# Attention's probabilities in units of 512 columns, and scores written further ahead of the values

## The chip, the cores and the metric

The kernel runs on one core of one Trainium2 chip. A core has a matrix engine (TensorE, shown as PE, and as PEld for its weight loads), a vector engine (DVE), a scalar engine (ACT), GpSimd (POOL) and SyncE (SP), which here issues most DMAs. The metric is the device time of one launch in microseconds; the time of a kernel is the median of its runs.

## The reference, cut to what matters

All arrays are float32; `x` is 2 sequences of 2048 tokens with 256 features. A feed-forward layer with three experts stands before and after a causal attention with one head of 128 features:

```python
x = x + 0.5 * _L0_ffn_ref(_layernorm(x), ...)      # three experts, one wins each token
x = x + _L0_attn_ref(_layernorm(x), Wq, Wk, Wv, Wo)
x = x + 0.5 * _L0_ffn_ref(_layernorm(x), ...)      # the same weights again

def _L0_attn_ref(x, Wq, Wk, Wv, Wo):
    Q = x @ Wq
    K = x @ Wk
    V = x @ Wv
    logits = jnp.einsum('bqd,bkd->bqk', Q, K) * d_k ** (-0.5)
    logits = jnp.where(causal, -jnp.inf, logits)
    attn = jax.nn.softmax(logits, axis=-1)
    out = jnp.einsum('bqk,bkd->bqd', attn, V)
    return out @ Wo
```

In the feed-forward layer each token's three bids are computed from a gated mix of its normalized row; the expert with the highest bid is applied to it. Experts 0 and 1 are squared-ReLU networks with 1024 hidden features, expert 2 is a gated product with 256.

## The kernel before, in words

A tile has 128 tokens, a group has 4 tiles (512 tokens), a sequence has 4 groups. The program is one long list that Python generators write out. Each generator yields between its steps, and a driver decides in which order steps of several generators are written. Tile, the layer that builds the program, then gives each engine its own order: it goes through the list with a model of the durations, the written order is the priority, and an instruction may be put on its engine ahead of others that were written earlier. On the chip each engine takes its instructions in the order that was fixed there. Two calls hold instructions in place: `tc.keep_in_program_order(ins)` keeps one in its written place, and `tc.issue_after(ins)` (in the helper `behind`) puts those of a block behind `ins` on that engine.

**The feed-forward layer.** `front` works through the 8 groups of the two sequences. For each it normalizes the rows (`start`, `norm1`, which writes the columns `YN` of the group's `rows` tile), transposes them (`columns`), multiplies (`r`, `v`, `mix`), computes the bids (`route`, `logits`), chooses the winner (`choose`, whose last decision is the `wins` at L525), ranks the tokens per expert and scatters the rows by indirect DMA to `by_slot` in DRAM (`move`). `experts` works on blocks of up to 256 gathered rows: SyncE loads the rows, `ready` updates them (on VectorE L975, on ScalarE L976), `columns` transposes them, `first` makes the hidden features, `second` multiplies back and scatters the result to DRAM. Blocks of expert 2 are of the kind `gt`; there `first` ends with the product `gated` (L994), which `back_to_rows` (L877) multiplies next. The experts of the first sequence are written between the steps of the second sequence's front. Toward the end of the first layer, `ahead` fetches the first sequence's rows back from `x_mid`, one of its steps to three of the experts', and `normed` normalizes them for attention; `moments` computes each group's statistics with four `bn_stats` (L281). With `landing`, the first of these four is kept in its written place.

**Attention.** It runs for one sequence at a time. For the first it is written alone; for the second its steps are written between those of the next layer's front, nine of the front for eight of attention's.

- `qkv` makes the projections, two steps for each of the 4 groups. The first sequence uses the `YN` columns of the four `rows` tiles as its normalized input (`normed`); the second normalizes into `xn`, with two buffers.
- `scores` makes the probabilities of one query tile a step. Tile i of group n has n + 1 key chunks of up to 512 columns. Each chunk is a matmul into a bank `ps_s` (L1125) of the pool `p_mm`, which has 6 banks, also used by projections and sums. The last chunk is masked (L1133). VectorE takes each chunk's maximum (L1134), then that of the row (L1137) and its shift (L1138); ScalarE writes the exponentials to `prob` (L1141) and their sums; VectorE adds these up (L1150) and inverts them (L1152). `prob` is a tile of 128 x 2048, with 5 buffers, whatever the group.
- `values` goes through the key blocks of 128, of which group n has 4(n + 1). For a block it transposes the four query tiles' probabilities (L1165) into a bank of `p_tp`, copies this to `p_tr` (on VectorE for even blocks, L1172, on ScalarE for odd ones, L1170) and multiplies by the block's values (L1178). The transposes and the copy of a block are written one block ahead of its multiplication. After the second block the group before is finished (`sums`: L1194, L1200, L1205), in two steps.

The end of `attention` sets the written order. The first group's four score tiles stand in the last four steps of `qkv`. Those of group n + 1 stand among the steps of the values of group n, one after every n + 1 steps:

```python
side = scores(n + 1, seq, following) if n + 1 < GB else iter(())
for i, _ in enumerate(values(n, seq, probs)):
    if i % (n + 1) == n:
        next(side, None)
    yield
```

Of the kernel before, what the change touches and what calls it, by code (L numbers as in the profile page):

```python
# [8 lines left out]
F32 = mybir.dt.float32  # L9
# [7 lines left out]
P = 128  # L17
# [61 lines left out]
def kernel(ctx: ExitStack, tc: tile.TileContext, a: dict, out: bass.AP):  # L79
# [196 lines left out]
    def moments(src, landing=False):  # L276

        stats = small.tile([P, TB, 6], F32, name="stats")
        mv = small.tile([P, TB, 2], F32, name="mv")
        for t in range(TB):  # L280
            ins = nc.vector.bn_stats(stats[:, t, :], src[:, t, :])  # L281
            if landing and t == 0:
                tc.keep_in_program_order(ins)
        for t in range(TB):
            nc.vector.bn_aggr(mv[:, t, :], stats[:, t, :])
        return mv
# [80 lines left out]

    groups = []


    RW_AT, GT_AT, HALF_AT, MORE_AT, STEER = accumulate(POS, POS, POS, SQ, 1)

    class Group:
# [136 lines left out]
        def choose(self):  # L510
            upto = self.seg["upto"]
            if self.n == 0 and self.seg["prior"] is not None:
# [11 lines left out]
            nc.vector.tensor_tensor(wins[:, 2, :], bids[:, 2, :], most[:, 0, :], ALU.is_gt)  # L524
            nc.vector.scalar_tensor_tensor(  # L525
                wins[:, 1, :], wins[:, 0, :], 1.0, wins[:, 2, :], ALU.is_lt, ALU.subtract
            )
            for t in range(TB):
# [300 lines left out]
    def experts(work, segs, dest, redo=None):  # L829
# [118 lines left out]
        class Block:  # L948
# [35 lines left out]

            def first(self, following=None):

                if self.kind == "gt":
# [3 lines left out]
                    if following:  # L991
                        following.ready()
                    self.mid = work.tile([P, KC, BLK], F32, name="gated", bufs=2)
# [21 lines left out]
        def pipelined(todo):  # L1015
# [7 lines left out]
            yield  # L1023
            todo[0].ready()
            todo[0].columns()
            yield
            for i, block in enumerate(todo):
                if i + 1 < len(todo):
                    todo[i + 1].load_weights()
                if i + 2 < len(todo):  # L1030
                    todo[i + 2].load_rows()
                yield from block.first(todo[i + 1] if i + 1 < len(todo) else None)
                if i + 1 < len(todo):
                    todo[i + 1].columns()
                    yield
                yield from block.second()
# [29 lines left out]

    def attention(work, x, normed=()):

        stat = work

        def qkv(made):
# [6 lines left out]
            def begin(n):  # L1078
                if len(norms) <= n < GB:
                    xn = work.tile([P, TB, C], F32, name="xn", bufs=2)  # L1080
                    norms.append((xn, normalize(xn, x[n])))
                    next(norms[n][1])
# [31 lines left out]

        def scores(n, seq, probs):

            for i in range(TB):
                qi = n * TB + i
                prob = work.tile([P, T], F32, name="prob", bufs=5)
                top = stat.tile([P, GB], F32, name="top", bufs=6)  # L1120
# [18 lines left out]
                sums = stat.tile([P, GB], F32, name="sums", bufs=6)  # L1139
                for c, (ps, w) in enumerate(parts):  # L1140
                    nc.scalar.activation(  # L1141
                        prob[:, c * TG : c * TG + w],
                        ps[:, :w],
                        AF.Exp,
# [5 lines left out]
                nc.vector.reduce_sum(total, sums[:, : n + 1], axis=AX.X)  # L1150
                inv = stat.tile([P, 1], F32, name="inv", bufs=10)
                nc.vector.reciprocal(inv, total)  # L1152
                probs.append((prob, inv))
                yield

        def values(n, seq, probs):
            ps_o = p_mm.tile([P, TG], F32, name="ps_o", tag="mm")
            blocks = (n + 1) * TB

            def keys_first(j):  # L1160
# [3 lines left out]
                for i in range(i0, TB):  # L1164
                    nc.tensor.transpose(  # L1165
                        ps[:, i * P : (i + 1) * P], probs[i][0][:, j * P : (j + 1) * P], ident
                    )
# [8 lines left out]
            for j in range(blocks):  # L1176
# [11 lines left out]
                yield  # L1188
            left.append(sums(n, ps_o, probs))

        def sums(n, ps_o, probs):

# [3 lines left out]
            for t0 in range(0, TB, 2):  # L1196
# [6 lines left out]
                for i in range(2):  # L1203
                    t = t0 + i
                    nc.vector.scalar_tensor_tensor(  # L1205
                        x[n][:, t, :], ps[:, i, :], probs[t][1], x[n][:, t, :], ALU.mult, ALU.add
                    )
            yield

        seq, probs, left = {}, [], []  # L1210

        first_scores = scores(0, seq, probs)
        for i, _ in enumerate(qkv(seq)):
            if i >= GB:
                next(first_scores)
            yield
        yield from first_scores
        for n in range(GB):
            following = []
            side = scores(n + 1, seq, following) if n + 1 < GB else iter(())  # L1220
            for i, _ in enumerate(values(n, seq, probs)):
                if i % (n + 1) == n:
                    next(side, None)
                yield
            yield from side
            probs = following
        yield from left.pop()
# [87 lines left out]
    with pool("attention", "right") as work:  # L1315
        for n in range(GB):
            x = front_pool.tile([P, TB, C], F32, name=f"x{n}")
            wait_for(nc.sync.dma_start(x, token_tiles(x_mid, GB + n)).ins, s0["results"] + s1["results"])
            t1["x"].append(x)
        run(attention(work, t0["x"], [r[:, :, YN : YN + C] for r in t0["rows"]]))  # L1320
        following = front(front_pool, [t0, t1], by_exp=GB)
        interleave(attention(work, t1["x"]), until_placed(following, t0), 9, 8)
        advance(following, AHEAD)
# [49 lines left out]
```

## Time and profile before

| what | value |
|---|---|
| time before, median of 3 runs | 892.63 us (891.55 to 897.54) |
| the profiled execution, its own time | 900.5 us |
| its span, first to last instruction | 898.5 us |
| mean granted TensorE clock | 0.988 |
| first sequence's attention on TensorE, first transpose to last product | about 342 to 467 us |
| second sequence's attention, with the next front | about 467 to 642 us |

The profile is one execution; busy times are per engine, and idle time is told for the instruction that ended it, with what released it. Start times are in us from the start of the span. A float32 matmul stands as two instructions in the records, a transpose as one; ends of matmuls are modelled, so the records of neighbouring matmuls overlap.

### The profile page before, as it was taken

The numbers are of one execution on the slowest core, as the hardware profiler recorded it, in microseconds if no ns is written. First come the engines' busy times: TensorE is split into PE (matmuls) and PEld (weight loads), VectorE is DVE, ScalarE is ACT, GpSimd is POOL, SyncE is SP. The second block draws the span as 40 slices with busy tenths as digits, with TensorE's granted clock in tenths as the row PEclk, the third lists the DMA queues.
The fourth block names the chain that finished last, engine by engine and source line by source line (L and its number), as shares of the span: only waits on it lengthen the run. The fifth ranks groups of instructions, "written<-read, shape, count | busy, mean of one in ns | idle before, by whom it ended". The sixth has DMA issues, their size and how long they took to land. (4 is left out here: it accounts for less than half of the span.)

```text
span 898.5 us, 12471 instructions
## 1 busy us (share of the span) xinstructions
PE 846.5 (94%) x4136; PEld 616.5 (69%) x4136; DVE 467.4 (52%) x1857; ACT 320.1 (36%) x694; POOL 184.8 (21%) x232
## 2 busy tenths in 40 slices
PE   6999899999999998899899999999899899999996
PEld 4556467788878895545456556556566688888885
DVE  3688757333345445478532687675776532333322
ACT  3332541324344332344533344442352223243221
POOL 3145245111032211000000102022323410122101
PEclk9999999999999999999999999999999999999998
DMA  9425637647188543000000001021375654539642
GB/s 308 150 102 194 224 142 264 216 136 264 49 293 296 171 142 100 0 1 1 0 1 1 1 0 71 24 95 42 127 279 182 242 191 161 177 95 333 199 164 70
DMA packets 66370, 123.71 MB, mean 138 GB/s; under 512 B 4718, under 2 KB 44526, under 8 KB 66288
## 3 DMA queue, kind: packets, MB, share of 16 engines
q1 hardware_dynamic: 55856, 87.46, 29.0%
q0 software_dynamic: 8384, 33.70, 9.5%
q10 hardware_dynamic: 2048, 1.58, 0.6%
q8 instruction: 37, 0.61, 0.3%
q14 instruction: 45, 0.37, 0.1%
HBM read 82.47 MB, written 38.68 MB: 135 GB/s over the span
## 5 line engine op out<-in xcount | busy, mean ns | idle before, releaser
L877 PE MATMUL acc<-w_e,hid 128*128 128x256 f32 x704 | 158.2, 382 | 0.0
L862 PE MATMUL ps_b<-cols,w_k 128*128 128x256 f32 (+1 forms) x768 | 157.3, 363 | 0.0
L862 PEld LDWEIGHTS ps_b<-cols,w_k 128*128 128x128 f32 x768 | 137.4, 191 | 17.1
L877 PEld LDWEIGHTS acc<-w_e,hid 128*128 128x128 f32 x704 | 132.7, 192 | 17.9 <-DVE hid L1004 0.6
L291 POOL TENSOR_TENSOR r<-ve,mhalf 128x4 f32<-128x4 f32 (+1 forms) x40 | 50.9, 1272 | 383.0 <-DVE ve L332 264.4
L1003 ACT ACTIVATE relu<-ps_b 128x512 f32<-128x512 f32 x88 | 52.0, 591 | 179.5 <-PE ps_b L862 155.9
L1004 DVE TENSOR_TENSOR hid<-ps_b,relu 128x512 f32<-128x512 f32 x88 | 60.8, 691 | 84.8 <-ACT relu L1003 79.3
L902 DVE SCALAR_TENSOR_TENSOR res<-acc,rows_in 128x256 f32<-128x256 f32 x68 | 30.0, 478 | 123.9 <-PE acc L877 123.9
L1178 PE MATMUL ps_o<-p_tr,v 128*128 128x512 f32 (+3 forms) x160 | 75.2, 554 | 4.7 <-DVE p_tr L1172 1.9
L567 POOL DMA_INDIRECT by_slot<-rows,slots x64 | 62.5, 977 | 32.0 <-issue 27.0
L1141 ACT ACTIVATE prob<-ps_s,shift 128x512 f32<-128x512 f32 (+2 forms) x80 | 49.0, 621 | 53.8 <-DVE shift L1138 44.5
L1125 PE MATMUL ps_s<-k_t,q_t 128*128 128x512 f32 (+3 forms) x160 | 64.8, 533 | 0.9 <-ACT prob L1141 0.9
L910 POOL DMA_INDIRECT out_dram<-res,where x34 | 33.6, 987 | 155.4 <-DVE res L902 142.3
L362 PE MATMUL ps_p<-y_t,w_r 128*128 128x512 f32 x128 | 63.5, 615 | 0.8 <-ACT y_t L416 0.7
L362 PE MATMUL ps_p<-y_t,w_v 128*128 128x512 f32 x128 | 62.2, 605 | 0.0
L910 POOL DMA_INDIRECT x_mid<-res,where x34 | 33.7, 992 | 133.2 <-DVE res L902 128.0
L442 PE MATMUL acc<-w_o,gate_t 128*128 128x256 f32 x256 | 60.1, 385 | 0.6 <-DVE gate_t L432 0.6
L1165 PEld LDWEIGHTS ps_pt<-ident,prob 128*128 128x128 f32 x272 | 34.1, 143 | 36.9 <-issue 18.8
L1134 DVE TENSOR_REDUCE top<-ps_s 128x1 f32<-128x512 f32 (+2 forms) x80 | 48.4, 607 | 17.2 <-PE ps_s L1125 15.8
L442 PEld LDWEIGHTS acc<-w_o,gate_t 128*128 128x128 f32 x256 | 47.1, 190 | 8.6 <-DVE gate_t L432 1.4
L1125 PEld LDWEIGHTS ps_s<-k_t,q_t 128*128 128x128 f32 x160 | 29.9, 193 | 32.8 <-issue 24.7
L354 ACT ACTIVATE cols<-ps_bt,lnp 128x256 f32<-128x256 f32 (+1 forms) x96 | 47.2, 554 | 13.2 <-PE ps_bt L846 12.9
(219 smaller groups left out, 1128.1 us busy)
## 6 DMA issues: line engine op xcount, KB each, us to landing
w_k<-in_K_rwkv_dram SPq DMA_DIRECT2D x24, 1024.0 KB, 5.3
w_e<-in_V_rwkv_dram SPq DMA_DIRECT2D x24, 1024.0 KB, 5.8
rows_in<-by_slot SPq DMA_DIRECT2D x20, 516.0 KB, 6.6
rows_in<-by_slot SPq DMA_DIRECT2D x12, 772.0 KB, 6.6
rows<-in_x_dram SPq DMA_DIRECT2D x8, 512.0 KB, 5.9
by_slot<-rows_in SPq DMA_DIRECT2D x3, 772.0 KB, 10.5
x_mid<-rows_in SPq DMA_DIRECT2D x1, 2048.0 KB, 15.8
rows<-x_mid SPq DMA_DIRECT2D x4, 512.0 KB, 5.1
```

The lines of the kernel that those rows point to most:

```text
L291: guess = nc.gpsimd.tensor_tensor(r0[:, 0:n, :], ve[:, 0:n, :], mhalf[:, 0:n, :], ALU.pow)
L362: nc.tensor.matmul(ps, lhsT=w[:, k, m * P : (m + 1) * P], rhs=src_t[:, k, :], start=k == 0, stop=k == KC - 1)
L442: nc.tensor.matmul(acc[:, i, :], lhsT=self.gate_t[:, k, t * P : (t + 1) * P], rhs=w_o[:, k, :], start=k == 0, stop=k == KC - 1,)
L567: nc.gpsimd.indirect_dma_start(out=by_slot, out_offset=bass.IndirectOffsetOnAxis(ap=self.slots[:, t : t + 1], axis=0), in_=self.rows[:, t, :],
L862: nc.tensor.matmul(ps[:, j, :], lhsT=w[:, k, (m0 + j) * P : (m0 + j + 1) * P], rhs=cols[:, k, :], start=k == 0, stop=k == KC - 1,)
L877: nc.tensor.matmul(acc[:, i, :], lhsT=src[:, j, i * P : (i + 1) * P], rhs=w[:, j, :], start=j == 0, stop=j == n - 1,)
L910: ins = nc.gpsimd.indirect_dma_start(out=dest, out_offset=bass.IndirectOffsetOnAxis(ap=where[:, i : i + 1], axis=0), in_=res[:, i, :], in_ ...
L1003: nc.scalar.activation(relu, ps, AF.Relu)
L1004: self.made = nc.vector.tensor_mul(self.mid[:, j : j + step, :], ps, relu).ins
L1125: nc.tensor.matmul(ps[:, :w], lhsT=seq["q_t"][:, qi * P : (qi + 1) * P], rhs=seq["k_t"][:, c * TG : c * TG + w], start=True, stop=True,)
L1141: nc.scalar.activation(prob[:, c * TG : c * TG + w], ps[:, :w], AF.Exp, bias=shift, scale=ATTN_SCALE, accum_out=sums[:, c : c + 1],)
L1178: nc.tensor.matmul(ps_o[:, i0 * P :], lhsT=seq["v"][:, j, :], rhs=p_tr[:, i0 * P :], start=j == 0, stop=j == blocks - 1,)
```

## The change

- The five whole rows `prob` become 20 tiles `prob0` to `prob19` of 128 x 512 (`units`), of the same size in all, shared by both sequences. `homes` gives each query tile of group n exactly n + 1 of them, or halves of other tiles: in the fourth group two query tiles use four pieces of `spare`. In the first sequence these are halves of the normalized rows of groups 0 and 1, in the second the two `xn` tiles.
- `scores` is one generator over all 16 query tiles. Six are written in `qkv`, from its third step on. The other ten are written at steps given as a list for the values of each group: three, four, three and none.
- `inv` has 12 buffers for 10.
- With `landing`, all four `bn_stats` are kept in their written place.
- `ready` for the first two blocks of `experts` is put behind the most recent `wins` of L525.

```diff
@@ moments
-            if landing and t == 0:
+            if landing:
                 tc.keep_in_program_order(ins)
@@ Group.choose
-            nc.vector.scalar_tensor_tensor(
+            lately["chosen"] = nc.vector.scalar_tensor_tensor(
                 wins[:, 1, :], wins[:, 0, :], 1.0, wins[:, 2, :], ALU.is_lt, ALU.subtract
-            )
+            ).ins
@@ Block.first, and pipelined
-            def first(self, following=None):
+            def first(self, following=None, early=False):
...
                     if following:
-                        following.ready()
+                        following.ready(lately["chosen"] if early else None)
...
-            todo[0].ready()
+            todo[0].ready(lately["chosen"])
...
-                yield from block.first(todo[i + 1] if i + 1 < len(todo) else None)
+                yield from block.first(todo[i + 1] if i + 1 < len(todo) else None, i == 0)
@@ attention
-    def attention(work, x, normed=()):
+    def attention(work, x, units, spare, normed=()):
+        homes = [[units[i : i + 1] for i in range(4)]]
+        homes.append([units[4 + 2 * i : 6 + 2 * i] for i in range(4)])
+        homes.append([units[12:15], units[15:18], units[18:20] + units[0:1], units[1:4]])
+        homes.append([units[4:8], spare[0:3] + units[8:9], spare[3:4] + units[9:12], units[12:16]])
...
-        def scores(n, seq, probs):
-            for i in range(TB):
-                qi = n * TB + i
-                prob = work.tile([P, T], F32, name="prob", bufs=5)
+        def scores():
+            for qi in range(T // P):
+                n, i = divmod(qi, TB)
+                home = homes[n][i]
...
                     nc.scalar.activation(
-                        prob[:, c * TG : c * TG + w],
-                        ps[:, :w],
+                        to[:, :w] if len(to.shape) == 2 else to,
+                        ps[:, :w] if len(to.shape) == 2 else ps.rearrange("p (a b) -> p a b", a=2),
...
-        first_scores = scores(0, seq, probs)
-        for i, _ in enumerate(qkv(seq)):
-            if i >= GB:
-                next(first_scores)
-            yield
-        yield from first_scores
-        for n in range(GB):
-            following = []
-            side = scores(n + 1, seq, following) if n + 1 < GB else iter(())
-            for i, _ in enumerate(values(n, seq, probs)):
-                if i % (n + 1) == n:
-                    next(side, None)
-                yield
-            yield from side
-            probs = following
+        seq, probs, left = {}, [[] for _ in range(GB)], []
+        tiles = scores()
+        for i, _ in enumerate(qkv(seq)):
+            if i >= 2:
+                next(tiles)
+            yield
+        for n, due in enumerate([(0, 1, 3), (0, 2, 4, 6), (1, 4, 10), ()]):
+            for i, _ in enumerate(values(n)):
+                if i in due:
+                    next(tiles)
+                yield
         yield from left.pop()
@@ the caller
-        run(attention(work, t0["x"], [r[:, :, YN : YN + C] for r in t0["rows"]]))
+        units = [work.tile([P, TG], F32, name=f"prob{u}") for u in range(5 * GB)]
+        xns = [work.tile([P, TB, C], F32, name=f"xn{i}") for i in range(2)]
+        normed_rows = [r[:, :, YN : YN + C] for r in t0["rows"]]
+        def halves(tiles):
+            return [t[:, i : i + 2, :] for t in tiles for i in range(0, TB, 2)]
+        run(attention(work, t0["x"], units, halves(normed_rows[0:2]), normed_rows))
         following = front(front_pool, [t0, t1], by_exp=GB)
-        interleave(attention(work, t1["x"]), until_placed(following, t0), 9, 8)
+        interleave(attention(work, t1["x"], units, halves(xns)), until_placed(following, t0), 9, 8)
```

## The prediction

> **What bounds the kernel now.** I read the page first, for the share of each engine:
>
> ```profile
> span 898.5 us, 12471 instructions
> PE 846.5 (94%) x4136; PEld 616.5 (69%) x4136; DVE 467.4 (52%) x1857; ACT 320.1 (36%) x694; POOL 184.8 (21%) x232
> ```
>
> TensorE is busy for 94% of the span, the next engine for 52%. Attention's arithmetic is the same before and after, so only TensorE's idle time can be won, 52 us in all, and only where this change touches what it waits for. Next I read the waits of TensorE between 371 and 467 us: the first batch's attention from its first values to its end, where no other TensorE work is mixed in. The columns are the total in us, the times, and the longest:
>
> ```profile
> PE ps_pt L1165 <- ACT prob L1141: 4.8, 5, 1.8
> PE ps_o L1178 <- DVE p_tr L1172: 1.4, 2, 0.7
> PE ps_s L1125 <- ACT prob L1141: 0.9, 1, 0.9
> PE ps_out L1200 <- ACT o_t L1194: 0.7, 1, 0.7
> PE ps_o L1178 <- DVE total L1150: 0.7, 1, 0.7
> PE ps_o L1178 <- ACT p_tr L1170: 0.6, 2, 0.3
> PE ps_pt L1165 <- ACT p_tr L1170: 0.6, 1, 0.6
> ```
>
> The largest line is the transposes of probabilities waiting for the exponentials, five times. The timeline shows the first (start, length, engine, line; in brackets the idle time and who ended it):
>
> ```profile
> 371.45 0.71 PE L1165 MATMUL ps_pt<-ident,prob 128*128 128x128 f32 x5
> 371.98 0.69 DVE L1134 TENSOR_REDUCE top<-ps_s 128x1 f32<-128x512 f32 x1
> 373.08 0.69 ACT L1141 ACTIVATE prob<-ps_s,shift 128x512 f32<-128x512 f32 x1 [3.50 <-DVE shift L1138]
> 373.92 0.44 PE L1165 MATMUL ps_pt<-ident,prob 128*128 128x128 f32 x2 [1.76 <-ACT prob L1141]
> 375.41 1.91 PE L1178 MATMUL ps_o<-p_tr,v 128*128 128x512 f32 x2
> ```
>
> The last query tile of a group has its scores just before the group's values begin. Its maximum on VectorE and exponential on ScalarE then stand between TensorE and the next transpose, and no scores fill the hole: four of the five probability buffers hold this group, the fifth the next group's first tile. The same stands at 385 us (idle 0.42 and 1.07), 409.5 (0.83) and 441 (0.70): the seams between groups. With the 1.76 these are the five waits of 4.8 us.
>
> The windows give a second cost. The first number after the busy times is the granted clock:
>
> ```profile
> 374.00:378.00 4.00, 3.43 (x8) 1.63 (x9) 1.33 (x4) 0.48 (x1) 0.00 (x0) 0.60 0.00 0
> 386.00:390.00 4.00, 2.26 (x6) 0.83 (x5) 1.42 (x7) 2.11 (x7) 0.00 (x0) 0.81 0.00 0
> 390.00:394.00 4.00, 4.00 (x12) 2.22 (x11) 1.38 (x2) 0.00 (x0) 0.00 (x0) 0.77 0.00 0
> ```
>
> After each of the first two seams the clock drops: 0.40 of 4 us is 1.6 us lost, and 0.19 and 0.23 of 4 us are 1.7. After the shorter waits at 409 and 441 it stays at 1.00.
>
> Last, I looked for the two other edits' waits, before attention:
>
> ```profile
> 99.98 0.43 DVE L975 SCALAR_TENSOR_TENSOR rows_in<-rows_in 128x256 f32<-128x256 f32 x1 [2.36 <-DMA rows_in<-by_slot]
> ...
> 101.72 0.36 PE L536 MATMUL ps_rank<-wins,before 128*128 128x12 f32 x2 [1.11 <-DVE wins L525]
> ...
> 257.15 1.08 DVE L281 BATCH_NORM_STATS2 stats<-rows 128x6 f32<-128x256 f32 x3 [3.06 <-DMA rows<-x_mid]
> ...
> 258.37 0.67 DVE L994 TENSOR_TENSOR gated<-ps_b,gt_sig 128x512 f32<-128x512 f32 x1
> ...
> 259.09 1.99 PE L877 MATMUL acc<-w,gated 128*128 128x256 f32 x8 [1.58 <-DVE gated L994]
> ```
>
> In both, VectorE's queue was blocked by an instruction whose DMA had not landed, while TensorE needed something behind it.
>
> **The change part by part.** The terms are for the profiled execution, 900.5 us around its span of 898.5. It is 0.9% above the median of the runs shown, 892.63; I carry the gain over in proportion.
>
> *All four statistics held in written order (L281).* Three of the first group's four ran at 257 us, in front of `gated`; the fourth, already held, ran at 284.7 among its neighbours. Moved there, they add 3 x 0.41 us to VectorE, which is idle for longer stretches around it while `acc` accumulates. TensorE's 1.58 us goes, and 0.16 more: five transposes stand as 0.71 us, so one follows another by 0.109 but the last is drawn 0.273 long, and a wait costs about 0.16 more than its idle time. Gain **1.7**, between 0 (another statistic blocks elsewhere) and 1.7.
>
> *`ready` behind `chosen` (L975).* Near 100 us the winner's choice no longer waits 2.36 us in the queue for rows. TensorE's waits there are 1.11 (ranks) and 0.56 (`acc` for `gate_t`), 2.0 with the overhang. Some returns: the rows' update still waits on the DMA, now behind L525, with `gate_t` (L432) and ScalarE's L976 behind it, and `sig` behind that. I take **1.5**, between 0 and 2.4 (the whole slip of TensorE's starts there). In the second layer the same wait is 0.49 us, with no idle TensorE of size behind it: nothing.
>
> *Units and order of the tiles.* Multiplications, reductions, exponentials and copies keep their number and sizes; a query tile takes as many 512-column units as it has key groups. So the first group needs 4 units, not 4 whole rows, and later groups' tiles have room early. The written order now begins six tiles within the projections, where it began four, and three, four and three within the values of the first three groups. So at every seam the last tile of the coming group lies one to five steps of values back; a step is four transposes and two 128x512 matmuls, 0.44 + 0.86 = 1.3 us from the starts. The last wait to cover is reduction, two small operations and exponential: 371.98 to 373.92, some 2 us. For the fourth group the reductions and exponentials are four each, but two more steps of values follow in which they run. I let all five waits go: 4.8 + 5 x 0.16 = 5.6, and both clock drops, 3.3: **8.9**. The bounds are 5 (the seam at 441 and one clock drop stay) and 8.9.
>
> [...]
>
> *Waits for the transposed copy* (`ps_o` and `ps_pt` on `p_tr`, and the one named `total`): 1.4 + 0.7 + 0.6 + 0.6 = 3.3, with six overhangs 4.3. The copy still takes 0.69 us after the transpose. At three seams a score tile of the next group may now fill it; at the last seam and in the last group nothing can. I take **1.8**, between 0 and 4.3. The 0.93 us of `ps_s` waiting for an exponential is a bank of PSUM coming free, which the change does not touch: 0.5, between 0 and 1.1.
>
> *Second batch.* The front of the next layer already fills its seams; between 467 and 642 us TensorE's waits for copies and `total` sum to 1.9 us. I take **1.0**, between 0 and 2.8.
>
> *What it adds.* Reductions come at another pace beside the copies of `p_tr` on VectorE. From 375 to 443 us VectorE is busy 47.1 of 68 us. About 4 us (two tiles) move ahead into the projections and some 10 us of TensorE's waits go: 43 of 56, 77%. I charge 1.0 us of new waits; the bounds are 0 and one 0.69 us reduction ahead of each of the 12 copies that VectorE makes in the first three groups, 8.3. The fourth group's second and third tiles stand in the normalized rows of groups 0 and 1, free since the projections. The next layer must not rewrite these before the last values: its normalizations, at 405.8 and from 429 us now, move to after some 457 us. Batch 2's projections hide this: the transposes that read them come at 474.15 and 506.81, so about 15 us of cover remain. Without it, the chain of root, scale and two 0.54 us activations, some 3 us, would show. No DMA is added or moved past SP's or POOL's queue. The tile that reuses units 4 to 7 waits for transposes just ahead of it on TensorE; behind its exponential on ScalarE stand copies for odd blocks, at most one block's 0.44 us, inside the bounds above.
>
> Sum: 1.7 + 1.5 + 8.9 + 1.8 + 0.5 + 1.0 - 1.0 = 14.4 us, or 1.6% of 900.5; 892.63 less 1.6% is **878.4**. All best ends: 1.7 + 2.4 + 8.9 + 4.3 + 1.1 + 2.8 = 21.2, giving 871.6. Poor ends: 5 - 8.3 = -3.3, slightly slower than before, at 896.
>
> **The rivals.**
>
> *The wait moves to PSUM.* Score tiles run ahead until all six banks are taken, and TensorE stands at `ps_s` as at 430 us. Eight tiles of the first batch have three or four chunks; 1.09 each is 8.7, so 14.4 - 8.7 = 5.7: **887.0**. For: the wait exists already. Against: once only, and the tiles are three to six steps apart.
>
> *It does not do what it says.* Engines' orders are settled at build time, with written order only a preference (statistics written for 284 us ran at 257). If scores stay where they are, the first two edits remain, 3.2: **889.5**. Against: the full buffers, which fixed the place of the scores, are gone.
>
> *VectorE becomes the bound beside the values, and it gets slower.* A tile's reductions (0.69 each) get in front of a copy of `p_tr`, and `ps_o` waits, 12 such copies in the first batch. At three reductions each, 2.07 x 12 = 24.8, less 14.4, is 10.4 slower: **903**. It decides from 1.2 us a copy. For: 8.74 of 10 us busy on VectorE from 400 to 410. Against: with the same mix, copies now cost TensorE 0.7 us at most, and all of it at seams.
>
> **How the numbers follow.** Forecast 0.62, PSUM 0.19, unchanged order 0.09, VectorE 0.10. The predicted time is the forecast's. The range reaches from just under the best ends, 870, past the two middle cases to 891; it leaves out the slower rival and a little more. A measurement here tells about 1% from no change: 883.7 and 901.6. Below lie the forecast and a part of PSUM's case, 0.70; above most of VectorE's, 0.08; 0.22 lies between.
>
> **What would show it.** Right: between the start and end of the first attention `ps_pt` hardly waits for `prob`, no half clock follows it, the stretch from 342 to 467 us is some 11 us shorter; `gated` no longer follows a late statistic, and L525 is not behind L975. Wrong: `ps_s <- ACT prob` or `ps_o <- DVE p_tr` grown to several us, or the two normalizations late at the second batch's projections.

## The result, and the profile after

The changed kernel took 881.04 us (median of 6 runs, 880.18 to 888.6) beside 893.73 us for the kernel before: a ratio of 0.9876, 95% interval 0.9829 to 0.9922. The forecast was 878.4 us, so 2.6 us too fast. A later measurement gave less: 895.14 beside 900.43 us, ratio 0.9938 (0.9917 to 0.9958). Both are faster, by 1.2% and by 0.6%; how much faster is not one number here, and a part of this document is about why.

The profiled execution took 888.6 us, 11.9 us less than the 900.5 us of before's; each is slower than the median of its kernel. In `after`, the helper lines moved by one: scores are L1141, exponentials L1158, transposes of probabilities L1182, values L1195, copies `p_tr` L1187 (ScalarE) and L1189 (VectorE), the update of the rows L976 and L977, `gated` L995. The page first:

```profile
span 886.4 us, 12466 instructions
PE 845.2 (95%) x4136; PEld 616.9 (70%) x4136; DVE 467.0 (53%) x1857; ACT 319.5 (36%) x694; POOL 184.8 (21%) x232
```

Every engine's busy time is what it was, within 1.3 us. The work is the same; only idle time of TensorE moved. The waits of TensorE between 368 and 456 us, again the first attention from its first values to its end:

```profile
PE ps_o L1195 <- DVE p_tr L1189: 1.4, 3, 0.7
PE ps_o L1195 <- ACT p_tr L1187: 1.2, 2, 0.6
PE ps_pt L1182 <- ACT prob L1158: 0.7, 1, 0.7
PE ps_o L1195 <- DVE shift L1153: 0.7, 1, 0.7
PE ps_pt L1182 <- ACT p_tr L1187: 0.7, 1, 0.7
PE ps_out L1217 <- ACT o_t L1211: 0.7, 1, 0.7
```

The line that was the longest has gone from 4.8 us in five waits to 0.7 in one, and the wait of a score tile for a PSUM bank (0.9) is not there. The waits for the transposed copy, which I had expected to shrink, stand: 4.0 us with the one named `shift` (before: 3.3 with the one named `total`). All lines together are 5.4 us, 4.3 less than before. The timeline of the first seam shows what is left of it:

```profile
370.46 0.93 PE L1182 MATMUL ps_pt<-ident,prob 128*128 128x128 f32 x7
...
371.10 0.69 DVE L1189 COPY p_tr<-ps_pt 128x512 f32<-128x512 f32 x1
371.43 0.48 ACT L1187 COPY p_tr<-ps_pt 128x384 f32<-128x384 f32 x1 [3.26 <-PE ps_pt L1182]
371.94 1.10 PE L1195 MATMUL ps_o<-p_tr,v 128*128 128x512 f32 x2 [0.55 <-ACT p_tr L1187]
372.54 0.69 ACT L1158 ACTIVATE prob<-ps_s,shift 128x512 f32<-128x512 f32 x1 [0.63 <-DVE shift L1154]
372.87 1.34 PE L1141 MATMUL ps_s<-k_t,q_t 128*128 128x512 f32 x3
```

Seven transposes of probabilities (the first two blocks) run without a wait: the exponentials were done. What TensorE waits for now is the copy of what it has just transposed. The exponential at 372.54 belongs to a later tile and delays nobody. The windows over the first two seams show the clock, the number after the busy times:

```profile
370.00:374.00 4.00, 3.45 (x15) 2.08 (x14) 2.33 (x8) 1.71 (x5) 0.00 (x0) 1.00 0.01 2
378.00:382.00 4.00, 3.32 (x19) 2.13 (x18) 3.37 (x14) 2.59 (x7) 0.00 (x0) 1.00 0.00 0
382.00:386.00 4.00, 4.00 (x15) 2.20 (x14) 2.51 (x7) 1.72 (x6) 0.00 (x0) 1.00 0.00 0
```

It stays at 1.00 from 344.54 us to the end of the first attention. From the start of its first query projection (342.07 us) to the start of its last output matmul the first attention takes 112.6 us; before, it took 120.2. Of these 7.6 us, 4.3 are waits and 3.3 the two clock drops. About 0.4 us goes the other way: half clock that began ahead of the stretch (a mean of 0.55 from 337 to 344.5 us) reaches 2.5 us into it, and before it reached 1.6 us. The 0.4 us left over is of the size of what four waits fewer save beyond their idle time.

The two smaller edits. Near 100 us the winner's choice (L525) now stands ahead of the update that waits for rows (L976), and TensorE reads the ranks without a wait (no bracket):

```profile
99.66 0.15 DVE L525 TENSOR_TENSOR wins<-bids,most 128x4 f32<-128x4 f32 x1
100.28 0.42 DVE L976 SCALAR_TENSOR_TENSOR rows_in<-rows_in 128x256 f32<-128x256 f32 x1 [0.26 <-DMA rows_in<-by_slot]
101.85 0.39 PE L537 MATMUL ps_rank<-wins,before 128*128 128x12 f32 x2
```

Near 257 us the statistics are gone from in front of `gated`, and so is the 1.58 us that TensorE waited for it. But the next block waits instead (TensorE first, then VectorE):

```profile
252.72 1.99 PE L878 MATMUL acc<-w,gated 128*128 128x256 f32 x8
...
259.36 0.33 PE L847 MATMUL ps_bt<-ident,rows_in 128*128 128x128 f32 x1 [1.19 <-ACT rows_in L977]
...
261.06 1.13 PE L878 MATMUL acc<-w,gated 128*128 128x256 f32 x4 [0.66 <-DVE gated L995]
...
258.25 0.76 DVE L976 SCALAR_TENSOR_TENSOR rows_in<-rows_in 128x256 f32<-128x256 f32 x2 [4.98 <-DMA rows_in<-by_slot]
```

VectorE is free for 4.98 us there, and its rows have not landed. From the `acc<-w,gated` that follows the earlier pair of blocks (246.42; before 251.19) to the first `acc<-w_e` of the blocks with a hidden layer (270.23; before 274.62) it takes 23.8 us, where it took 23.4: the whole gain was given back within one block.

### The profile page after: what moved, and what is told of

Its sections match the earlier page's. It is cut to its first block, busy times and chain, and to the rows that moved or that the text cites. A ratio compares the mean times of both kernels' runs of the same rounds, so it can differ in the third digit from the quotient of the medians.

```text
span 886.4 us, 12466 instructions
## 1 busy us (share of the span) xinstructions
PE 845.2 (95%) x4136; PEld 616.9 (70%) x4136; DVE 467.0 (53%) x1857; ACT 319.5 (36%) x694; POOL 184.8 (21%) x232
## 3 DMA queue, kind: packets, MB, share of 16 engines
q10 hardware_dynamic: 2048, 1.58, 0.6%
## 5 line engine op out<-in xcount | busy, mean ns | idle before, releaser
L1195 PE MATMUL ps_o<-p_tr,v 128*128 128x512 f32 (+3 forms) x160 | 73.4, 544 | 6.1 <-DVE p_tr L1189 2.9
L1141 PE MATMUL ps_s<-k_t,q_t 128*128 128x512 f32 (+3 forms) x160 | 64.2, 529 | 0.0
L1158 ACT ACTIVATE prob<-ps_s,shift 128x512 f32<-128x512 f32 (+3 forms) x72 | 43.6, 615 | 43.5 <-DVE shift L1154 43.5
L1141 PEld LDWEIGHTS ps_s<-k_t,q_t 128*128 128x128 f32 x160 | 29.1, 190 | 28.8 <-issue 25.8
L281 DVE BATCH_NORM_STATS2 stats<-rows 128x6 f32<-128x256 f32 x128 | 46.2, 411 | 5.4 <-DMA rows<-in_x_dram 5.4
```

What stands on the lines that cost most here:

```text
L1141: nc.tensor.matmul(ps[:, :w], lhsT=seq["q_t"][:, qi * P : (qi + 1) * P], rhs=seq["k_t"][:, c * TG : c * TG + w], start=True, stop=True,)
L1195: nc.tensor.matmul(ps_o[:, i0 * P :], lhsT=seq["v"][:, j, :], rhs=p_tr[:, i0 * P :], start=j == 0, stop=j == blocks - 1,)
```

## The experiments

Each ratio is against runs of the kernel before on the same chip. These fell on two levels: 893.7 to 893.8 us in the first measurement and the last four experiments, 900.4 us in the first eight. Experiments 1 to 4 ran on one chip, 5 to 8 on a second, 9 to 12 on a third, and the chip of the first measurement is not on record; so a level may be a chip's, and no run here separates the two. Times are therefore compared within a level, or by their ratios. "First attention" is the stretch of the 7.6 us above.

**1. The statistics alone.**

```diff
-            if landing and t == 0:
+            if landing:
```

> The kernel before with one edit: all four statistics of a landing group are held in their written place. Theory: the three statistics no longer block VectorE at 257 us, so the product of the gated block starts on time there (its wait of 1.58 us goes), but the rows of a later block, loaded 8 us earlier by SyncE, land no sooner, and TensorE waits for them instead; within two blocks all is given back and the time is the same within 0.5 us of that of before. Rival: the 1.7 us of the prediction's step stay, and every later mark of the trace is 1.7 us earlier. The traces tell it: the shift of the blocks' products after 265 us.

Measured: 901.88 us, ratio 1.0017 (0.9991 to 1.0043). `gated` no longer waits in the first of the two blocks; in the next, TensorE waits 1.98 us for the rows' update. No gain shows, with the mechanism seen in the changed kernel.

**2. `ready` behind `chosen` alone.**

```diff
+            lately["chosen"] = nc.vector.scalar_tensor_tensor(
...
+            todo[0].ready(lately["chosen"])
...
+                yield from block.first(..., i == 0)
```

> The kernel before with one edit: the first two blocks' row updates stand behind the latest choice of winners. Theory: TensorE's waits for the ranks and for gate_t near 100 us (1.1 and 0.6 us) go and do not come back, some 1.5 to 2.5 us in the first layer, nothing in the second; time 0.2 to 0.3% shorter. Rival A: the step is worth nothing, because the rows land as late and the next chain waits for them. Rival B: the 2 to 5 us that the trace after gained later, where TensorE had waited for ScalarE's rows_in near 159 and 709 us, belong to this edit too; then those waits are gone here as well and the gain is 6 us or more.

Measured: 898.6 us, ratio 0.9985 (0.9962 to 1.0008). Between the first routing's counts (L598) and the first block's transposes (L847) it takes 26.0 us; in experiments 1 and 3, without the edit, 26.6. In the ten other runs with it the same stretch took 25.3 to 26.2. So it is worth 0.4 to 1.3 us there, and no more than the time can show.

**3. The attention alone** (the changed kernel without these two edits).

```diff
-            if landing:
+            if landing and t == 0:
...
-            todo[0].ready(lately["chosen"])
+            todo[0].ready()
```

> The changed kernel without the other two edits: only attention's units and the new written order. Theory: this is most of the change. From the first projection to the last output product of the first attention it takes about 112.6 us as in the changed kernel, against 120.2 before; the second attention is not shorter; near 100 us and 257 us the waits of before are back. Time some 7 to 10 us under before, a ratio of about 0.990. Rival: the attention is worth less than half of that, and the rest of the changed kernel's gain stands in the feed-forward layers (the waits near 159 and 709 us that were gone in its trace); then the time is within 4 us of before.

Measured: 895.79 us, ratio 0.9957 (0.9936 to 0.9978). The first attention takes 112.2 us; in experiments 1 and 2, which keep the old attention, 118.1 and 118.0. The second attention takes 170.4 us against their 169.2 and 169.1. So the attention's gain stands by itself, and some of it is given back in the second batch.

**4. The units with the old written order.**

```diff
-            if i >= 2:
+            if i >= GB:
...
-        for n, due in enumerate([(0, 1, 3), (0, 2, 4, 6), (1, 4, 10), ()]):
+        for n, due in enumerate([(0, 1, 2, 3), (1, 3, 5, 7), (2, 5, 8, 11), ()]):
```

> The changed kernel with its units, but the score tiles written at the steps where the kernel before had them (four in the last four steps of the projections, then one after every n + 1 steps of the values). Theory: buffers alone don't suffice, since the last tile of a group is still written just before its group's values: the wait for the exponential at the seams comes back at least at the first two, some 3 us with the clock drops behind them, so half or more of the attention's gain is lost; first attention 116 to 120 us. Rival: the full buffers were all that held the scores; with them gone the build puts scores ahead by itself, and the first attention takes 112 to 114 us as in the changed kernel.

Measured: 900.41 us, ratio 1.0012 (0.9986 to 1.0039). The waits of TensorE in the first attention, from 368 to 462 us:

```profile
PE ps_pt L1182 <- ACT prob L1158: 5.0, 5, 1.8
PE ps_o L1195 <- DVE p_tr L1189: 1.3, 2, 0.7
```

All five waits at the seams are back, and one clock drop after them:

```profile
385.60:388.90 3.30, 3.30 (x8) 1.78 (x7) 0.69 (x1) 0.00 (x0) 0.00 (x0) 0.50 0.00 0
```

Only the score tile's wait for PSUM stays away. The first attention takes 116.9 us, 1.2 less than in experiments 1 and 2. So the buffers that allow another order bring about 1 us by themselves, which the times don't show; the written order brings the rest of the gain.

**5. The changed kernel again**, unedited, at the level of experiments 1 to 8.

> The changed kernel once more, beside the runs of this chip. Theory: the change is worth the seams of the first attention and the one wait for the ranks, about 5.6 us there (the first attention 112 to 113 us against 118 to 120) plus 1 to 1.7 us at the start, less 1.4 us given back in the second attention and nothing from the held statistics: some 4.5 to 6 us, a ratio of 0.9935 to 0.995. The rest of the first measurement's 0.9876 was then chance: in the changed kernel's first trace TensorE does not wait for the rows' transposed copy near 159 and 709 us (1.5 and 2.5 us, a clock drop each), and the trace of this run shows those waits again. Rival: those waits go away because of the change (its instructions lie elsewhere), so both are missing again and the ratio is 0.986 to 0.989.

Measured: 895.14 us, ratio 0.9938 (0.9917 to 0.9958). First attention 111.4 us, second 170.0. What differs from the first profile of the same program is two waits of TensorE for ScalarE (total, times, longest). In the first profile:

```profile
PE ps_bt L847 <- ACT rows_in L977: 1.4, 2, 1.2
...
PE ps_t L348 <- ACT by_col L479: 0.2, 1, 0.2
```

and in this one:

```profile
PE ps_bt L847 <- ACT rows_in L977: 8.1, 6, 3.3
...
PE ps_t L348 <- ACT by_col L479: 3.3, 3, 2.6
```

Together 9.8 us more, where the spans differ by 7.9; the first profile had one wait of 2.0 us for `gate_t` that this one has not. Near 155 us one sees where the wait comes from. The changed kernel in the first profile, then in this one:

```profile
154.59 0.60 ACT L1004 ACTIVATE relu<-ps_b 128x512 f32<-128x512 f32 x1 [1.13 <-PE ps_b L863]
```

```profile
157.49 0.60 ACT L1004 ACTIVATE relu<-ps_b 128x512 f32<-128x512 f32 x1 [5.01 <-remote]
...
151.68 3.62 PE L863 MATMUL ps_b<-cols,w_k 128*128 128x256 f32 x16
```

In the second, ScalarE idles 5.01 us in front of the same activation, while TensorE has written all its sums by 155.30 and stops; the trace names no engine of this core as the releaser. It was due at 153.61, one step of 1.73 us (0.60 and 1.13) after the one before it. Such pauses, by which an activation starts 2 to 4 us late (near 155, 637 and 705 us), are in each profile at the level of 900.4 us, save that experiment 7 has none near 637 and only about 1 us at a time near 705, and in none of the five profiles at 893.7. They go with the level and not with the change. The profile of before shows them too (4.3 us of `rows_in`, 3.2 of `by_col`), and its 900.5 us fits that level: the pair of profiles that the first section compares mixes both levels. In before's profile half clock follows the wait of 2.48 us near 709 us (0.50 from 712.8 to 716 us), but not that of 1.53 near 159 us (1.00 from 160.5 to 337 us).

**6. The fetches of the next layer's inputs later in the written order.**

```diff
-        advance(main, 6)
+        advance(main, 12)
```

> The changed kernel with the fetches of the second layer's inputs queued six steps later in the feed-forward. Theory 1: the held statistics took the gated product's wait away (1.6 us near 257), and the rows of the next block come too late by the DMA to make use of it, because the x_mid fetches share the DMA with them; with the fetches later the wait for the rows near 258 to 261 (1.2 to 2.1 us) shrinks below 0.5 us and the kernel gains 1 to 1.5 us on the changed kernel, a ratio 0.0015 lower. Rival: the rows are late for another reason (their gather starts late, on its own queue): the wait stays over 1 us and the time is unchanged, or the later inputs make the next attention's start late and cost 1 us or more after the feed-forward.

Measured: 896.26 us, ratio 0.9943 (0.9922 to 0.9963); the wait for the rows near 262 us is 0.83 us (1.01 in experiment 5). This was a miss of the experiment: SyncE's order is settled at build time, and the fetches stood at the same place in its queue. It led to experiment 10. In the changed kernel's first profile SyncE does this (its waits, then its timeline):

```profile
SPq L152 <- DMA x_mid<-res,where: 4.5, 1, 4.5
```

```profile
248.36 1.47 SPq L152 DMA_DIRECT2D rows<-x_mid  x3
250.16 0.38 SPq L933 DMA_DIRECT2D rows_in<-by_slot  x1
```

It waits 4.5 us for scattered results to land, then issues three fetches whose statistics run from 280.31 us on, and then the rows for which VectorE waits until 258.25.

**7. A score tile inside the copy's wait.** One more step in the values, after the first transposes of a group, and score tiles due at it:

```diff
             ahead = keys_first(0)
+            yield
...
-        for n, due in enumerate([(0, 1, 3), (0, 2, 4, 6), (1, 4, 10), ()]):
+        for n, due in enumerate([(0, 2, 4), (0, 3, 5, 7), (0, 5, 11), ()]):
```

> The changed kernel with one more step in the values, between the first transposes of a group and the second ones, and the score tiles due at (0, 2, 4), (0, 3, 5, 7), (0, 5, 11): a score tile is written where TensorE waits for the first transposed copy. Theory: each seam's wait for that copy (0.5 to 0.9 us each, 8 in the first attention, 5.2 us in all by the changed kernel's trace) falls at three of four seams, and the first attention is 1 to 2 us shorter than the changed kernel's 112.2 to 112.6 us. Rival 1: the score tile's own waits (VectorE's maximum, which stands ahead of the copy on VectorE) make the copy later, and the first attention is the same to 1 us longer. Rival 2: the waits are not at the seams but wherever VectorE's queue holds the copy up, and nothing changes within 0.5 us.

Measured: 887.3 us, ratio 0.9841 (0.9803 to 0.9879), 7.8 us less than the changed kernel at the same level. The first attention takes 109.8 us, 1.6 us less than in experiment 5; first to last value 77.3 us against 80.2. The rest is in the second batch and the front beside it: from its first query projection to the second routing's counts (L598 at 688.91) it takes 229.8 us against 235.1. Not all of that need be the step's doing: the pause near 637 us, for which TensorE waits 2.6 us in experiment 5 with a half clock after it (a mean of 0.79 from 638 to 646 us), is missing in this profile.

**8. The old order in the second attention alone.**

```diff
-        interleave(attention(work, t1["x"], units, halves(xns)), ...
+        interleave(attention(work, t1["x"], units, halves(xns), (), GB), ...
```

(with the start of the score tiles and their due lists as parameters; the first attention has the new order, the second the lists of experiment 4).

> The changed kernel with the old written order of the scores in the second attention alone. Theory: the new order costs 1.3 to 1.5 us in the second attention (170.4 against 168.9 us; there the feed-forward's steps fill the seams already, and the scores moved forward only bunch VectorE's work), so that attention takes 168.5 to 169.2 us and the kernel is 1.3 us faster than the changed kernel, a ratio 0.0015 lower; the first attention stays at 112 to 113 us. Rival: the 1.4 us came from the units or from where the feed-forward's steps fell, and the second attention stays at 170 us or more.

Measured: 893.91 us, ratio 0.9922 (0.9894 to 0.9949); the second attention takes 168.5 us against 170.0 in experiment 5. The waits of TensorE there, in experiment 5 and in this one:

```profile
PE ps_o L1195 <- DVE p_tr L1189: 1.5, 4, 0.6
PE ps_pt L1182 <- DVE total L1167: 0.8, 1, 0.8
PE ps_o L1195 <- ACT p_tr L1187: 0.8, 2, 0.5
```

```profile
PE ps_o L1195 <- DVE total L1167: 0.7, 1, 0.7
PE ps_o L1195 <- ACT p_tr L1187: 0.6, 2, 0.5
PE ps_o L1195 <- DVE p_tr L1189: 0.3, 1, 0.3
```

So the new order costs the second attention 1.5 us, most of it in waits for copies. The time went down by 1.2 us, as expected, but the intervals overlap: the traces show this, the times alone would not.

**9. The extra step in the first attention alone**, with the due lists of experiment 7 there.

```diff
             ahead = keys_first(0)
+            if early:
+                yield
```

> The changed kernel with the extra step and its due lists in the first attention alone; the second attention and all else as the change left them. Theory: the seams of the first attention are worth 2.9 us there (first to last value 77.3 us against 80.2, as in the run with both attentions), and the rest of that run's gain of 7.8 us came from the second attention, where the extra steps hand more of the front's steps to it: so this kernel gains 2 to 3 us on the changed kernel, 892 to 893.5 us beside 895.1. Rival: the first attention's own gain is most of it (through a clock drop that it avoids), and the time is within 2 us of 887.3.

Measured: 880.8 us beside 893.81, ratio 0.986 (0.9832 to 0.9889); this run fell on the other level, so its time stands beside the first measurement's 881.04 and not beside 895.1. The first attention's values take 77.3 us against 80.2, as in experiment 7. The waits for copies from 364 to 452 us:

```profile
PE ps_o L1197 <- DVE p_tr L1189: 1.0, 2, 0.7
PE ps_o L1197 <- DVE shift L1153: 0.7, 1, 0.7
PE ps_o L1197 <- ACT p_tr L1187: 0.6, 1, 0.6
```

2.3 us (2.5 with a 0.2 of `ps_out`) where the changed kernel has 4.0. The rest of the 2.9 us is score tiles that moved ahead of the first values; the whole first attention is 2.0 us shorter (110.6). The times can't show 2 us across two levels.

**10. The fetches behind the rows in SyncE's queue.**

```diff
+        with behind(lately["row_load"] if after else None):
+            ins = nc.sync.dma_start(seg["x"][n], src).ins
...
+            lately["row_load"] = ins
...
-        advance(main, 6)
+        advance(main, 12)
```

> The changed kernel with each fetch of the second layer's inputs placed behind a later block's row load in SyncE's queue (the run that only took them later in the written order left that queue as it was). Theory: in the changed kernel SyncE waits 4.5 us for the scattered results ahead of the first fetch and then issues three fetches (1.5 us), with the next block's row load behind them; the rows land some 6 us late for a VectorE that would be free, which is what gave the held statistics' 1.6 us back. With the load ahead, TensorE's wait for the rows near 258 to 262 us (1.0 to 1.2 us) goes, the one for the gated product there stays at 0.7 or goes, and the kernel gains 1 to 2 us on the changed kernel: 893 to 894 us. Rival: the rows' DMA shares the engines with the 2 MB of weights issued right behind it, lands as late as before, and nothing changes within 0.5 us; or the fetches, now later, make the next layer's normalizations late and the wait at the first projection near 341 us grows.

Measured: 883.54 us, ratio 0.9887 (0.9862 to 0.9912). SyncE, then VectorE and TensorE, up to 257 us:

```profile
241.17 6.66 SPq L934 DMA_DIRECT2D rows_in<-by_slot  x2
248.02 1.02 SPq L946 DMA_DIRECT2D w_k<-in_K_rwkv_dram  x1
...
251.52 0.43 DVE L978 SCALAR_TENSOR_TENSOR rows_in<-rows_in 128x256 f32<-128x256 f32 x1 [0.71 <-DMA rows_in<-by_slot]
...
256.96 1.99 PE L879 MATMUL acc<-w,gated 128*128 128x256 f32 x8 [0.41 <-DVE gated L997]
```

TensorE's 1.19 us for the rows is gone, and VectorE waits 0.71 us for them where it waited 4.98. Counted from the first `acc<-w,gated` of the stretch below, their load is issued after 3.1 us (at 247.46 us), where it was after 3.7 (at 250.16 us). It lands 4.0 us after its issue; in the changed kernel it took 8.1 us, behind the three fetches, which landed at 252.1, 254.9 and 256.9 us. So the rows come 4.7 us sooner, 0.6 by the earlier issue and 4.1 because no fetch is under way ahead of them. The stretch of 23.8 us (from the `acc<-w,gated` at 244.36 to the `acc<-w_e` at 266.13) takes 21.8. So the cause is shown: the fetches ahead of the rows held back what the statistics had given. The time does not show the 2.0 us: against the first measurement's ratio of 0.9876 the intervals overlap almost wholly.

**11. Both: the extra step and the fetches behind the rows.**

> The extra step in both attentions (887.3 us when run before) and the fetches behind the rows, together: the candidate for the fastest. If the two gains add, 885.5 to 887 us, a ratio of 0.982 to 0.984; if the rows' wait is not what held the stage, 887 to 888.

Measured: 876.27 us beside 893.81, ratio 0.9805 (0.9779 to 0.983): the fastest of all kernels here, and outside the interval of experiment 9. The 885.5 to 887 us expected were for the other level; by its ratio it did a little better than the 0.982 to 0.984. First attention 110.1 us, the stretch behind the statistics 21.8 us. Its waits for copies over the whole span:

```profile
PE ps_o L1198 <- DVE p_tr L1191: 1.3, 3, 0.7
...
PE ps_o L1198 <- ACT p_tr L1189: 1.1, 2, 0.6
```

Their sum is 2.4 us; the changed kernel's first profile has 2.9 and 2.3 us in these two lines.

**12. The front's steps faster beside the second attention.**

```diff
-        interleave(attention(...), until_placed(following, t0), 9, 8)
+        interleave(attention(...), until_placed(following, t0), 6, 5)
```

> The changed kernel with the front's steps handed out 6 for every 5 of the second attention's instead of 9 for 8, which is about what the extra step of a group does to their pace (60 attention steps in place of 56 give 67.5 front steps against 63; 6 for 5 gives 67). Nothing in the order of scores and values is changed. Theory: the pace is what gained 5.3 us in the second attention and the routing behind it (TensorE's wait of 2.6 us for by_col near 637 us went, with the half clock after it), so this kernel shows by_col's wait under 1 us and gains 4 to 5.5 us on the changed kernel, 889.5 to 891 us. Rival: it was the score tiles inside the copies' waits, and the time is within 1 us of the changed kernel's 895.1.

Measured: 883.75 us, ratio 0.9887 (0.9859 to 0.9914). Inconclusive: at this level ScalarE's pause before `by_col` isn't there at all (0.2 us in the changed kernel), so its removal couldn't be tested. From the second attention's first query projection to the second routing's counts this kernel takes 232.4 us, the changed kernel 235.1 (first profile), experiments 9 and 10 233.4 and 234.5, experiment 11 228.7. The pace alone brings 1 to 2.7 us of the 5.3; why the extra step brings more in the second batch stays open.

## Why the prediction was right, and where it was not

The forecast's time was near and its sign right; its terms are worth going through, for they did not come out as its sum did. The measured values are differences of the stretches above. The stretch from 342 to 467 us, for which some 11 us had been said, is 7.5 us shorter.

- **Seams, 8.9 us (bounds 5 to 8.9): right.** Four of five waits and both clock drops went: 4.1 us and 3.3 us, 7.4 without the small overhangs. The one at 441 us stayed, as the lower bound had allowed (0.7 us at 429 now). Experiment 4 shows that it is the written order which does it. In before's profile half clock came twice at the seams (0.50 from 374.8 to 378.2 and from 388.5 to 391.8 us), in experiment 4's, with five waits of 5.0 us, once (0.50 from 385.6 to 388.9 us), in the changed kernel's first not at all (1.00 from 344.6 to 450 us). In experiments 1 and 2 the five waits are 4.8 us as in before's, and the first attention is 2.1 and 2.2 us shorter, about one drop's 1.7. So the 3.3 us can also be 1.7.
- **PSUM, 0.5: the wait of 0.9 us went wholly**, though the prediction had it as untouched. The units alone remove it (experiment 4), for what reason was not tested; the rival in which this wait grows did not happen at all.
- **Transposed copies, 1.8 (bounds 0 to 4.3): wrong in sign, -0.7.** I had argued that a score tile of the next group may fill each wait. It could not: in the written order the tile comes after the step, and the wait is inside the first step, between the first transposes and the first values. Experiments 7 and 9 put a step there, and then the wait goes at three seams, for 2 us. The step that failed is "may now fill it"; I had not looked at where in a step a tile is written.
- **Second batch, 1.0 (0 to 2.8): wrong in sign, -1.5.** Its seams had little left to fill, as the prediction's own 1.9 us said; the new order cost more than that. This is the added cost that I had put at 1.0 for both batches, and it fell here. Experiment 8 shows it, mostly in waits for copies; that reductions moved beside the copies are the reason is argued, not shown.
- **Held statistics, 1.7 (0 to 1.7): the wait went, the gain did not come.** The step that failed is "TensorE's 1.58 us goes", priced as a gain without asking what is late next: the next block's rows were late by their DMA, and the trace of before showed it, VectorE idle for 2.99 us in front of `rows_in`, behind the `gated` I had priced. Experiments 1 and 10 show it: 0 alone, 2.0 us with the fetches out of the way.
- **`ready` behind `chosen`, 1.5 (0 to 2.4): right in kind**, 0.4 to 1.3.
- **VectorE becomes the bound: did not happen.** Waits for its copies in the first attention stayed at 1.4 us. VectorE's 77% beside the values was a slip of the sum: 43 of 58 us are 74%. The next layer's normalizations moved, to 429 to 447 us and not past 457, and stayed hidden, as forecast.

The first attention can also be estimated without the chance of the clock: take half of the time at half clock off each stretch (four transposes take 0.85 us at half clock, from 390.07 us in before's profile, and 0.44 at full, from 556.00 us). That leaves 116.0 to 116.1 us in the three profiles with whole rows, 115.2 with the units in the old order (experiment 4), 111.4 in all seven with the new order, and 109.3 in the three with the extra step. So by this estimate the units are worth 0.9 us, the order 3.8 and the extra step 2.1; the clock adds 1.7 us for each drop at a seam.

Put together: 7.6 us for the first attention (seams, PSUM and copies), -1.5 for the second, 0 and about 0.9 for the two edits make 7.0 us, where the sum said 14.4. The 5.3 us of experiment 5 lie nearer to that than the 12.7 of the first measurement. In the pair of profiles, the rest of the 11.9 us is about what TensorE waits behind ScalarE's pauses in before's (1.5, 2.5 and 2.5 us, less the 2.0 us for `gate_t` in after's); what the first measurement's medians owe to them is open, since no trace of before exists at that level. So the nearness of 878.4 to 881.04 is partly luck: two terms had the wrong sign and one was given back, and what sets the level of a run made up for it. What I would keep from it is the seams' term and its bounds; the small terms were each a hope that a wait would be filled, and only PSUM's was.

## What to carry to other kernels

To fill a wait of an engine, look where in the written step it falls: score tiles written after the step left TensorE's waits for copies at 4.0 us, and one extra `yield` inside it took them to 2.3 and was worth 2 us. Before pricing the removal of a stall, read what the same block waits for next, and what stands ahead of that request on its DMA queue; three fetches for later, issued just ahead of a load for now, made it land in 8.1 us for 4.0. Price a change from traces at one level of the unchanged kernel: the same program differed by 14 us between two, which may be two chips'.

## What the runs showed of the hardware that I had not expected

**The clock fell after short waits, in pieces of one length.** In the records of the granted clock in before's profile and the changed kernel's first, half clock stands, but for the last microseconds of a run, in pieces of 3.41 us, or two in a row. They start at 149.5, 344.1, 374.8, 388.4 and 712.7 us in before's and at 92.0, 337.7 (two), 644.9 and 692.7 us in the changed kernel's; the distances between the starts are 57, 9, 4 and 95 times this length, and 72, 90 and 14 times. One comes after a wait of 1.50 us (changed kernel, first profile: the wait before 690.86 us; busy times, then the clock):

```profile
688.50:692.50 4.00, 2.50 (x17) 2.06 (x17) 3.20 (x22) 1.25 (x3) 3.09 (x4) 1.00 0.64 256
693.00:696.00 3.00, 3.00 (x8) 2.37 (x8) 3.00 (x25) 0.00 (x0) 1.77 (x2) 0.50 0.57 218
696.50:699.50 3.00, 3.00 (x15) 2.64 (x15) 1.58 (x9) 1.19 (x2) 2.39 (x3) 1.00 0.93 247
```

TensorE was idle for 1.5 of the 4 us before it. A piece costs half of 3.41, 1.7 us, as an estimate from the transposes' 0.85 us at half clock for 0.44. In experiment 5 two waits of 1.01 and 0.66 us were followed by one (at 265.7 us; eight matmuls from 265.45 us take 3.62 us, where eight from 257.30 take 1.99), while a wait of 1.49 us near 145 us in the changed kernel's first profile was not (1.00 from 146.8 to 160 us). At the first seam in before's profile waits of 1.76 and 0.57 us were enough. What decides stays open.

**ScalarE paused with no visible cause.** At the level of 900.4 us a ScalarE activation began up to 4 us late (157.49 for 153.61 in experiment 5), at the same two or three places in all kernels; at the other level it did not. TensorE's waits for `rows_in` were 3.7 to 8.5 us in the eight experiments at the first and 0.5 to 1.7 us in the five profiles at the other. What holds it, and what sets the level, the chip or something else, stays open.
